# Three reorderings around the stage borders of a state-space, attention and mixture-of-experts kernel

## The chip, the cores and the metric

The kernel runs on one core of a Trainium2 chip. The metric is the device time of one execution in microseconds (us), as the median of several runs. Engine names are those of the profile: PE is TensorE (PEld its weight loads), DVE is VectorE, ACT is ScalarE, POOL is GpSimd, SP is SyncE, which here only issues DMAs.

## What is computed

Two layers, on 4 images of 1024 tokens with 256 channels. Layer 0 normalizes, projects to 512 channels, convolves by depth and runs a state-space recurrence with 64 states a channel along the tokens of each image:

```python
def step(h, inp):
    xt, dtt, Bt, Ct = inp
    dA = jnp.exp(dtt[:, :, None] * A)
    h = dA * h + (dtt * xt)[:, :, None] * Bt[:, None, :]
    y = jnp.einsum('bdn,bn->bd', h, Ct)
    return (h, y)
```

Layer 1 is a linear attention over each image and then a mixture of 16 experts, of which each token uses two, with the weights of their softmax scores:

```python
top_probs, top_idx = jax.lax.top_k(probs, 2)
top_probs = top_probs / jnp.sum(top_probs, axis=-1, keepdims=True)
dispatch = jnp.sum(jax.nn.one_hot(top_idx, n_experts) * top_probs[..., None], axis=-2)
hidden = jax.nn.silu(h1) * h2          # h1 = x @ w1[e], h2 = x @ w2[e]
expert_out = jnp.einsum('bseh,eho->bseo', hidden, w3)
```

## The kernel before

**Stage one, the recurrence** (to about 2698 us of the profiled execution). The work is cut into 8 units (an image's half, 512 tokens) and 64 states a unit, so 512 steps, each of 4 chunks of 128 channels. For each chunk `scan` (L946) runs one VectorE scan over 512 tokens into a ring of four states `h`. After the fourth chunk one GpSimd product (L961) multiplies all four chunks by the state's row of C, 128x2048 at once. `add_up` (L968) lets TensorE transpose the product into the sum `y` in PSUM, four transposes a chunk; it is issued 11 chunks behind the scan (LAG, L1090). The order on every engine is the order in which the loop at L1108 issues: nothing reorders it. After the last chunk `close_sum` (L988) copies `y` out, on VectorE and ACT in turn.

**Stage two, attention** (to about 2943 us). Its first instructions are a memset of `none` on GpSimd (L1240), its store by SP (L1241) and, behind that on SP's queue, the loads of the token tiles `tbs` (L1243 on). The order of this stage is written out by hand, image by image. At its end the expert inputs `xe` of the last image are normalized on ACT (`expert_in`, L1479) and stored by SP into the row table `xd` (L1494), the first three gathers of rows from `xd` are issued on GpSimd (`fetch_rows`, L1776), and the last image's scores are still to be made.

**Stage three, the experts.** Tokens are sorted into blocks of 128 rows, each of one expert. Three blocks an expert are fixed (48); 25 more come from a list made in this stage, and more still would come behind a condition. `blocks_of` (L2050) runs over 73 blocks. For a block: `fetch_rows` gathers its rows (up to seven blocks ahead, `look_ahead`, L2056), `turn_rows` (L1983) transposes them on TensorE (px) and copies them on ACT to xT, `hidden` (L2000) makes two halves of the first products (16 TensorE instructions each, L2008), ACT's Silu and VectorE's product hT (L2015), `result` (L2019) makes the second product, and `put_result` (L2028) scales it and adds it to the output by a scattering DMA from GpSimd. SP loads the experts' weights up to four blocks ahead.

Before the first block, `blocks_of` issues in this order: weight loads, gathers, then `turn_e` (L1496: eight transposes of the first half of xe and two ACT copies to xeT) and `gates` (L1504: four score products and one ACT copy), and then `turn_rows` of the first block.

Between the halves of a block, `on_with` (L1660) advances a chain of generators by four steps (one step after the first eight blocks). A step runs to the next `yield`. The chain is: the second half of the last scores and its routing (`rest_of_routing`, L2095), `spare_rows` (L2109), `more_places` (L2114) and `more_rows` (L2156). `more_places` counts the blocks beyond the fixed ones: `ef` on VectorE, a TensorE transpose of it (L2135), and from that the experts' numbers `eid` (L2136), which SP reads when it loads weights for a listed block. `more_rows` makes the list itself, in eight groups: for each, VectorE compares (`ih`, L2165) and multiplies (`code`, L2171), ACT fills the other half of `code` (L2175), then a `yield`, and eight small TensorE products (L2180) add the group to one PSUM tile. When all are in, `sources` (L1704) turns the sums into row numbers and `choices` (L1717) prepares the weights of the rows.

Of the kernel before, what the change touches and what calls it, by code (L numbers as in the profile page):

```python
# [9 lines left out]
BF16 = mybir.dt.bfloat16  # L10
I32 = mybir.dt.int32
AF = mybir.ActivationFunctionType
ALU = mybir.AluOpType
# [3 lines left out]
P = 128  # L17
BANK = 512
# [15 lines left out]
def conv_ssm_attn_moe_kernel(ctx: ExitStack, tc: tile.TileContext, a: dict, out: bass.AP):  # L34
    nc = tc.nc
# [7 lines left out]
    NE, _, HID = a["L1_ffn_w1"].shape  # L43
    NT = L // P
    NTA = NB * NT
    CK = C // P
    DK = DN // P
# [9 lines left out]
    NMORE = 2 * NB * L // BS - 2 * (FIX - 1)  # L57
# [16 lines left out]
    ident = const.tile([P, P], F32, name="ident")  # L74
# [56 lines left out]
    def blk(i, n=BANK):  # L131
        return slice(i * n, (i + 1) * n)
# [12 lines left out]
    with ExitStack() as l0:  # L145
# [64 lines left out]
        for m in range(DK):  # L210
            for ck in range(CK):
                nc.tensor.matmul(
                    pbi[:, m : m + 1], w_in[:, ck, blk(m, P)], b1[:, ck : ck + 1],
                    start=(ck == 0), stop=(ck == CK - 1),
# [42 lines left out]
        made = {}  # L257
# [616 lines left out]
        steps = [(u, n) for u in range(len(units)) for n in range(NS)]  # L874
# [71 lines left out]
        def scan(s, m):  # L946
            u, n = steps[s]
            b, seg = units[u]
            if m == 0:
                made["h", s] = ring[:, s % RING, :, :]  # L950
            if seg == 0 and n == 0 and m == 0:
                last[b] = acts.tile([P, NS, DK], F32, name="last", bufs=1)
            h = made["h", s]
            nc.vector.tensor_tensor_scan(  # L954
                h[:, m, 1:], made.pop(("da", s, m)), made.pop(("dbx", s, m)),
                0.0 if seg == 0 else last[b][:, n, m : m + 1],
                ALU.mult, ALU.add,
            )
            if m == DK - 1:

                nc.gpsimd.tensor_tensor(  # L961
                    h[:, :, :BANK], h[:, :, 1:], over_middle(made["c", s], DK), ALU.mult
                )
                if seg + 1 < NHALF:
                    with nc.allow_non_contiguous_dma(reason="one element a partition"):
                        nc.sync.dma_start(out=last[b][:, n, :], in_=h[:, :, BANK])
# [126 lines left out]
        with tc.manual_schedule():  # L1093
# [14 lines left out]
            for k in range(n_all + LAG):  # L1108
# [29 lines left out]
                while True:  # L1138
                    best = None
                    for i, l in enumerate(lists):  # L1140
                        if not l or ready[i] + l[0][1] > k or l[0][0] > at and i != holds:
                            continue
                        when, _, eng, c, _, pb, need = l[0]
# [11 lines left out]
                    _, _, eng, c, what, pb, _ = lists[i].pop(0)  # L1155
# [43 lines left out]
    qh = l1.tile([P, 2, NTA, BS], BF16, name="qh")  # L1199
# [493 lines left out]
    eid = late.tile([1, NMORE], I32, name="eid")  # L1693
# [97 lines left out]
    steps = iter(())  # L1791
    for o in range(NB):
        n = o + 1 if o + 1 < NB else None
        z = o - 1 if o > 0 else None
        s = o + 2 if o + 2 < NB else None
# [56 lines left out]
        if z is not None:  # L1852
            turn_g(z)
            steps = route(z)
# [70 lines left out]
    rt2 = ctx.enter_context(tc.tile_pool(name="rt2", bufs=2))  # L1925
# [11 lines left out]
    def one():  # L1937
        return ps_c.tile([P, BANK], F32, name="one", tag="po")
# [44 lines left out]
    def turn_rows(key):  # L1983
        px = ps_x.tile([P, CK, BS], F32, name="px")
        for ck in range(CK):
            nc.tensor.transpose(px[:, ck, :], on_b["xb", key][:, blk(ck, P)], ident)
        xT = ffn.tile([P, CK, BS], F32, name="xT")
        nc.scalar.copy(xT, px)  # L1988
        on_b["xT", key] = xT
# [60 lines left out]
    def blocks_of(todo, beside=(), fast=0, fetched=0):  # L2050

        beside = iter(beside)
        n = len(todo)
        rows = fetched

        def look_ahead(i, deep):  # L2056
            nonlocal rows
            while rows < min(i + deep, n) and todo[rows][0] in given_rows:
                fetch_rows(todo[rows])
                rows += 1  # L2060

        homes.clear()
        held = 0

        def load_ahead(i, gone):
            nonlocal held
            while held < min(i + AHEAD, n) and fetch_weights(todo, held, gone):
                held += 1

        load_ahead(0, 0)  # L2070
        look_ahead(0, AHEAD)
        if fast:
            turn_e(NB - 1, 0)
            gates(NB - 1, 0)
        turn_rows(todo[0])
        for i in range(n + 1):
            if i < n:
                look_ahead(i, 7)
                hidden(todo[i], 0)
            on_with(beside, 4 if i < fast else 1)  # L2080
            if i > 0:
                result(todo[i - 1], 2)
                put_result(todo[i - 1])
            load_ahead(i, i)
            assert i == n or held > i
            if i + 1 < n:
                turn_rows(todo[i + 1])
            if i < n:
                hidden(todo[i], 2)
                weigh(todo[i])  # L2090
                result(todo[i], 0)
            on_with(beside, 4 if i < fast else 1)
        on_with(beside, 99)
# [20 lines left out]
    def more_places():  # L2114

        nbi = rt.tile([P, NE], I32, name="nbi")
        nc.vector.tensor_scalar(nbi, counts[-1], float(BS - 1), None, ALU.add)
        nc.vector.tensor_single_scalar(nbi, nbi, BS.bit_length() - 1, ALU.arith_shift_right)
        nb = rt.tile([P, NE], F32, name="nb")
        nc.vector.tensor_scalar(nb, nbi, -float(FIX), None, ALU.add)  # L2120
        nc.vector.tensor_scalar(nb, nb, 0.0, None, ALU.max)
        nc.vector.tensor_tensor_scan(
            places_to, every[:, :NE], nb, 0.0, ALU.mult, ALU.add
        )
        nc.vector.tensor_scalar(
            used_i, places_to[:, NE - 1 :], 1.0, None, ALU.add
        )
        nc.vector.tensor_tensor(places_of, places_to, nb, ALU.subtract)
        yield
        done = rt.tile([P, NE], F32, name="done")  # L2130
        nc.vector.tensor_scalar(done, places_to, block_p, None, ALU.is_le)
        ef = rt.tile([P, 1], F32, name="ef")
        nc.vector.tensor_reduce(ef, done, AX.X, ALU.add)
        pe = one()
        nc.tensor.transpose(pe[:1, :P], ef, ident)  # L2135
        nc.vector.tensor_scalar(eid, pe[:1, :NMORE], float(NE - 1), None, ALU.min)  # L2136
        yield
        bf = rt.tile([P, 2 * NTA], F32, name="bf")
        for k in range(4):
            pick = rt2.tile([P, NTA // 2, NE], F32, name="pick")  # L2140
            hot = hot_all.rearrange("p k g e -> p (k g) e")[:, blk(k, NTA // 2), :]
            nc.vector.tensor_tensor(pick, hot, over_middle(places_of, NTA // 2), ALU.mult)
            nc.vector.tensor_reduce(bf[:, blk(k, NTA // 2)], pick, AX.X, ALU.add)
            yield
        inside = within.rearrange("p k g -> p (k g)")
        few = rt.tile([P, 2 * NTA], F32, name="few")
        nc.vector.tensor_scalar(
            few, inside, float(FIX), 4.0 * P, ALU.is_lt, ALU.mult
        )
        nc.vector.scalar_tensor_tensor(  # L2150
            bf, inside, -float(FIX), bf, ALU.add, ALU.add
        )
        nc.vector.tensor_tensor(bh, bf, few, ALU.add)
        yield

    def more_rows(lo, hi):  # L2156

        n = hi - lo
        GC = NTA // 4
        pg = one()[:, : 2 * n].rearrange("p (s n) -> p s n", s=2)  # L2160
        for k in range(2):
            for c in range(NTA // GC):
                gs = slice(c * GC, (c + 1) * GC)
                ih = rt2.tile([P, GC, n], BF16, name="ih", tag=f"ih{n}")
                nc.vector.tensor_tensor(  # L2165
                    ih, over_middle(blocks_h[:, lo:hi], GC),
                    over_last(bh[:, k * NTA + c * GC : k * NTA + (c + 1) * GC], n),
                    ALU.is_equal,
                )
                code = rt2.tile([P, GC, 2, n], BF16, name="code", tag=f"code{n}")  # L2170
                nc.vector.tensor_tensor(  # L2171
                    code[:, :, 0, :], ih,
                    over_last(groups[:, c, 0, :], n), ALU.mult,
                )
                nc.scalar.activation(  # L2175
                    code[:, :, 1, :], ih, AF.Copy, scale=part_pk[:, k : k + 1]
                )
                yield
                for j in range(GC):
                    nc.tensor.matmul(  # L2180
                        pg.rearrange("p s n -> p (s n)"), qh[:, k, c * GC + j, :],
                        code[:, j, :, :].rearrange("p s n -> p (s n)"),
                        start=(k + c + j == 0),
                        stop=(k == 1 and (c + 1) * GC + j == NTA + GC - 1),
                    )
        lo, hi = NFIX + lo, NFIX + hi
        nc.vector.tensor_copy(low[:, lo:hi], pg[:, 1, :])
        sources(lo, hi, pg[:, 0, :], low[:, lo:hi])
        given_rows.update(range(lo, hi))
        yield  # L2190
        choices(lo, hi)
        yield
# [57 lines left out]
```

## Time and profile before

| | us |
|---|---|
| Median of 3 runs | 3376.29 (3375.55 to 3376.74) |
| The profiled execution | 3389.96, its span 3387.8 |
| Granted TensorE clock, mean | 0.988 of full |
| Last scan ends, last product of `h` and C starts | 2691.9, 2692.05 |
| First gather issued, first expert product starts | 2943.48, 2951.14 |
| List: first and last group of L2180 start | 2994.3, 3004.9 |
| Last scattering DMA issued | 3376.91 |

Times in a profile count from the span's start. A timeline line gives start, length, engine, line of the code, operation, output and inputs with their shapes, how many instructions are merged, and in brackets how long the engine stood idle before and who ended that. A line of waits gives who waited for whom, the total in us, how often, and the longest. A line of stretches gives the busy time of each engine and the clock that TensorE was granted.

The sum of busy shares is of little use here, since most of the span is stage one: what an edit at a stage border does is read from the timeline there.

### The profile page before, as it was taken

The numbers are of one execution on the slowest core, as the hardware profiler recorded it, in microseconds if no ns is written. First come the engines' busy times: TensorE is split into PE (matmuls) and PEld (weight loads), VectorE is DVE, ScalarE is ACT, GpSimd is POOL, SyncE is SP. The second block draws the span as 40 slices with busy tenths as digits, with TensorE's granted clock in tenths as the row PEclk, the third lists the DMA queues.
The fourth block names the chain that finished last, engine by engine and source line by source line (L and its number), as shares of the span: only waits on it lengthen the run. The fifth ranks groups of instructions, "written<-read, shape, count | busy, mean of one in ns | idle before, by whom it ended". The sixth has DMA issues, their size and how long they took to land. (4 is left out here: it accounts for less than half of the span.)

```text
span 3387.8 us, 62750 instructions
## 1 busy us (share of the span) xinstructions
PE 3172.2 (94%) x23407; PEld 2753.3 (81%) x23407; DVE 2886.9 (85%) x3435; ACT 2717.3 (80%) x4621; POOL 2718.4 (80%) x1215
## 2 busy tenths in 40 slices
PE   7899999999999999999999999989999889789998
PEld 4588888988898888888988988768778756589998
DVE  4699999999999999999999999999999867652222
ACT  1699999999999999999999999899999754322221
POOL 0488998999999989999998999899999842234443
PEclk9999999999999999999999999999999999999999
DMA  3552224224333332253334223423222210467785
GB/s 105 150 68 63 68 66 69 71 71 62 67 78 69 68 72 76 62 63 74 73 73 68 71 64 60 71 54 68 60 62 67 80 48 29 156 186 231 214 245 149
DMA packets 423835, 300.76 MB, mean 89 GB/s; under 512 B 225073, under 2 KB 329393, under 8 KB 423522
## 3 DMA queue, kind: packets, MB, share of 16 engines
q1 hardware_dynamic: 397202, 274.25, 32.9%
q0 software_dynamic: 14016, 18.05, 2.8%
q10 hardware_dynamic: 12304, 4.37, 0.5%
q8 instruction: 187, 3.06, 0.4%
q14 instruction: 126, 1.03, 0.1%
HBM read 262.34 MB, written 34.87 MB: 88 GB/s over the span
## 5 line engine op out<-in xcount | busy, mean ns | idle before, releaser
L961 POOL TENSOR_TENSOR h<-h,cb_n 128x2048 f32<-128x2048 f32 x512 | 2154.9, 4226 | 142.6 <-DVE h L954 89.9
L928 ACT ACTIVATE da<-dt,l_conv_a_log_sb 128x512 f32<-128x512 f32 x2048 | 1438.3, 714 | 32.4 <-DVE h L954 31.3
L908 ACT ACTIVATE bx<-dtxT,proj 128x512 f32<-128x512 f32 x1748 | 1246.9, 714 | 29.9 <-DVE dtxT L600 16.4
L975 PE MATMUL y<-ident,h 128*128 128x128 f32 x8192 | 1236.5, 274 | 8.9 <-POOL h L961 5.8
L954 DVE TENSOR_TENSOR_SCAN h<-da,last,ps 128x512 f32<-128x512 f32 x1024 | 1217.9, 1262 | 7.0 <-PE ps L940 1.8
L954 DVE TENSOR_TENSOR_SCAN h<-da,ps 128x512 f32<-128x512 f32 x1024 | 1169.8, 1201 | 41.8 <-DMA last<-h 16.8
L940 PE MATMUL ps<-ident,bx 128*128 128x128 f32 x6992 | 1119.0, 276 | 41.7 <-DVE h L954 29.4
L975 PEld LDWEIGHTS y<-ident,h 128*128 128x128 f32 x8192 | 979.0, 141 | 99.9 <-issue 20.6
L940 PEld LDWEIGHTS ps<-ident,bx 128*128 128x128 f32 x6992 | 819.7, 142 | 101.8 <-DVE h L954 81.1
L2015 DVE TENSOR_TENSOR hT<-s,p 128x256 f32<-128x256 f32 x146 | 61.4, 421 | 281.0 <-ACT s L2014 281.0
L940 PE MATMUL ps<-ident,bxp 128*128 128x128 f32 x800 | 237.6, 297 | 58.9 <-DVE h L954 46.0
L2033 POOL DMA_INDIRECT out_dram<-yb,src x73 | 116.0, 1589 | 212.3 <-DVE yb L2030 82.2
L2014 ACT ACTIVATE s<-p 128x256 f32<-128x256 f32 x146 | 56.1, 384 | 265.4 <-PE p L2008 262.6
L413 PE MATMUL bg<-pad,dgc 128*128 128x256 f32 x864 | 258.2, 380 | 0.4 <-DMA dgc<-diags 0.4
L940 PEld LDWEIGHTS ps<-ident,bxp 128*128 128x128 f32 x800 | 112.3, 140 | 142.0 <-DVE h L954 89.2
L919 POOL TENSOR_SCALAR bxp<-dtxT,proj 128x512 f32<-128x512 f32 x200 | 147.0, 735 | 59.5 <-DVE dtxT L600 59.5
L935 PE MATMUL ps<-dgb,dtxT 128*128 128x128 f32 x800 | 170.3, 295 | 22.5 <-DMA dgb<-diag_b 9.7
L2008 PE MATMUL p<-xT,w 128*128 128x128 f32 x1408 | 171.7, 275 | 2.2 <-ACT xT L1988 2.2
L2008 PEld LDWEIGHTS p<-xT,w 128*128 128x128 f32 x1408 | 167.4, 192 | 5.0 <-ACT xT L1988 2.9
L935 PEld LDWEIGHTS ps<-dgb,dtxT 128*128 128x128 f32 x800 | 120.5, 190 | 49.2 <-DVE h L954 36.2
L413 PEld LDWEIGHTS bg<-pad,dgc 128*128 128x128 f32 x864 | 130.5, 191 | 0.7 <-DMA dgc<-diags 0.7
L2008 PE MATMUL p<-xT,m 128*128 128x128 f32 x928 | 115.4, 278 | 0.0
(341 smaller groups left out, 2681.6 us busy)
## 6 DMA issues: line engine op xcount, KB each, us to landing
cb_n<-cd SPq DMA_DIRECT2D x512, 256.0 KB, 3.3
m<-in_L_ffn_w_dram SPq DMA_DIRECT2D x87, 512.0 KB, 5.6
w<-in_L_ffn_w_dram SPq DMA_DIRECT2D x60, 512.0 KB, 6.9
dgc<-diags SPq DMA_DIRECT2D x84, 192.0 KB, 3.1
diag_b<-zero SPq DMA_DIRECT2D x2, 4096.0 KB
dgb<-diag_b SPq DMA_DIRECT2D x100, 64.0 KB, 3.2
last<-h SPq DMA_DIRECT2D x256, 2.0 KB, 3.1
xd<-xe SPq DMA_DIRECT2D x8, 512.0 KB, 3.5
```

The lines of the kernel that those rows point to most:

```text
L413: nc.tensor.matmul(made["bg"].rearrange("p (h w) -> p h w", w=WW)[:, blk(c, deep), :], made["dgc", m * 3 + i][:, j, :], pads[m][:, at : at ...
L908: nc.scalar.activation(t, made["dtxT", u][:, j, :], AF.Copy, scale=made["proj", u][:, j, R + n : R + n + 1])
L919: nc.gpsimd.tensor_scalar(t, made["dtxT", u][:, 0, :], made["proj", u][:, 0, R + n : R + n + 1], 1.0, ALU.mult, ALU.mult,)
L928: nc.scalar.activation(t, made["dt", u][:, m, :], AF.Exp, scale=A[:, m, n : n + 1])
L935: nc.tensor.matmul(t[:, blk(j, P)], made["dtxT", steps[s][0]][:, j, blk(m, P)], made["dgb", s], start=True, stop=True,)
L940: nc.tensor.transpose(t[:, blk(j, P)], made["bx", s, j][:, blk(m, P)], ident)
L954: nc.vector.tensor_tensor_scan(h[:, m, 1:], made.pop(("da", s, m)), made.pop(("dbx", s, m)), 0.0 if seg == 0 else last[b][:, n, m : m + 1] ...
L961: nc.gpsimd.tensor_tensor(h[:, :, :BANK], h[:, :, 1:], over_middle(made["c", s], DK), ALU.mult)
L975: nc.tensor.matmul(made["y", u][j][:, blk(m, P)], made["h", s][:, m, blk(j, P)], ident, is_transpose=True, start=n == 0 and m == 0, stop=n ...
L2008: nc.tensor.matmul(p12[:, j, s, :], w_of(w, key)[:, ck, blk(h + j, P)], on_b["xT", key][:, ck, :], start=(ck == 0), stop=(ck == CK - 1),)
L2015: nc.vector.tensor_tensor(on_b["hT", key][:, h : h + 2, :], s, p12[:, :, 1, :], ALU.mult)
L2033: s = nc.gpsimd.indirect_dma_start(of[:, :], bass.IndirectOffsetOnAxis(src[:, c : c + 1], 0), yb, None, bounds_check=NB * L - 1, oob_is_er ...
```

## The change

Three edits. (1) In the last of the 512 steps the product with C is made chunk by chunk, behind each scan: the even chunks on GpSimd, the odd ones on VectorE. (2) In `blocks_of` the first block's rows are transposed ahead of `turn_e` and `gates`. (3) In `more_rows` a group's products are issued three steps behind its code, with five buffers for `code` in place of two and one more `yield`; in `more_places` the transpose for `eid` moves behind the second of the four picks.

```diff
@@ -956,7 +956,11 @@
                 0.0 if seg == 0 else last[b][:, n, m : m + 1],
                 ALU.mult, ALU.add,
             )
-            if m == DK - 1:
+            if s + 1 == len(steps):
+                (nc.vector if m % 2 else nc.gpsimd).tensor_tensor(
+                    h[:, m, :BANK], h[:, m, 1:], made["c", s], ALU.mult
+                )
+            elif m == DK - 1:
 
                 nc.gpsimd.tensor_tensor(
                     h[:, :, :BANK], h[:, :, 1:], over_middle(made["c", s], DK), ALU.mult
@@ -2069,10 +2073,10 @@
 
         load_ahead(0, 0)
         look_ahead(0, AHEAD)
+        turn_rows(todo[0])
         if fast:
             turn_e(NB - 1, 0)
             gates(NB - 1, 0)
-        turn_rows(todo[0])
         for i in range(n + 1):
             if i < n:
                 look_ahead(i, 7)
@@ -2131,9 +2135,6 @@
         nc.vector.tensor_scalar(done, places_to, block_p, None, ALU.is_le)
         ef = rt.tile([P, 1], F32, name="ef")
         nc.vector.tensor_reduce(ef, done, AX.X, ALU.add)
-        pe = one()
-        nc.tensor.transpose(pe[:1, :P], ef, ident)
-        nc.vector.tensor_scalar(eid, pe[:1, :NMORE], float(NE - 1), None, ALU.min)
         yield
         bf = rt.tile([P, 2 * NTA], F32, name="bf")
         for k in range(4):
@@ -2141,6 +2142,12 @@
             hot = hot_all.rearrange("p k g e -> p (k g) e")[:, blk(k, NTA // 2), :]
             nc.vector.tensor_tensor(pick, hot, over_middle(places_of, NTA // 2), ALU.mult)
             nc.vector.tensor_reduce(bf[:, blk(k, NTA // 2)], pick, AX.X, ALU.add)
+            if k == 1:
+                pe = one()
+                nc.tensor.transpose(pe[:1, :P], ef, ident)
+                nc.vector.tensor_scalar(
+                    eid, pe[:1, :NMORE], float(NE - 1), None, ALU.min
+                )
             yield
         inside = within.rearrange("p k g -> p (k g)")
         few = rt.tile([P, 2 * NTA], F32, name="few")
@@ -2153,11 +2160,24 @@
         nc.vector.tensor_tensor(bh, bf, few, ALU.add)
         yield
 
+    LATE = 3
+
     def more_rows(lo, hi):
 
         n = hi - lo
         GC = NTA // 4
         pg = one()[:, : 2 * n].rearrange("p (s n) -> p s n", s=2)
+        behind = []
+
+        def add_rows(k, c, code):
+            for j in range(GC):
+                nc.tensor.matmul(
+                    pg.rearrange("p s n -> p (s n)"), qh[:, k, c * GC + j, :],
+                    code[:, j, :, :].rearrange("p s n -> p (s n)"),
+                    start=(k + c + j == 0),
+                    stop=(k == 1 and (c + 1) * GC + j == NTA + GC - 1),
+                )
+
         for k in range(2):
             for c in range(NTA // GC):
                 gs = slice(c * GC, (c + 1) * GC)
@@ -2167,7 +2187,9 @@
                     over_last(bh[:, k * NTA + c * GC : k * NTA + (c + 1) * GC], n),
                     ALU.is_equal,
                 )
-                code = rt2.tile([P, GC, 2, n], BF16, name="code", tag=f"code{n}")
+                code = rt2.tile(
+                    [P, GC, 2, n], BF16, name="code", tag=f"code{n}", bufs=LATE + 2
+                )
                 nc.vector.tensor_tensor(
                     code[:, :, 0, :], ih,
                     over_last(groups[:, c, 0, :], n), ALU.mult,
@@ -2176,13 +2198,12 @@
                     code[:, :, 1, :], ih, AF.Copy, scale=part_pk[:, k : k + 1]
                 )
                 yield
-                for j in range(GC):
-                    nc.tensor.matmul(
-                        pg.rearrange("p s n -> p (s n)"), qh[:, k, c * GC + j, :],
-                        code[:, j, :, :].rearrange("p s n -> p (s n)"),
-                        start=(k + c + j == 0),
-                        stop=(k == 1 and (c + 1) * GC + j == NTA + GC - 1),
-                    )
+                behind.append((k, c, code))
+                if len(behind) > LATE:
+                    add_rows(*behind.pop(0))
+        yield
+        for one_code in behind:
+            add_rows(*one_code)
         lo, hi = NFIX + lo, NFIX + hi
         nc.vector.tensor_copy(low[:, lo:hi], pg[:, 1, :])
         sources(lo, hi, pg[:, 0, :], low[:, lo:hi])
```

## The prediction

> **What bounds the kernel now.** I read the page's busy shares first, then the stretches by engine from 2940 us on, where two of the three edits act, then TensorE's waits there, and last the timelines around each edit.
>
> ```profile
> PE 3172.2 (94%) x23407; PEld 2753.3 (81%) x23407; DVE 2886.9 (85%) x3435; ACT 2717.3 (80%) x4621; POOL 2718.4 (80%) x1215
> 3100.00:3350.00 250.00, 250.00 (x1903) 238.38 (x1902) 70.23 (x226) 51.72 (x136) 120.37 (x136) 1.00 0.80 232
> PE one L2180 <- ACT code L2175: 4.9, 7, 1.7
> PE pgT L1510 <- ACT xeT L1281: 3.3, 1, 3.3
> ```
>
> The second line is a stretch of the expert stage: length, then busy time of PE, PEld, DVE, ACT, POOL, then granted clock, DMA share, GB/s. TensorE is busy 250.00 of 250 us, at full clock, with no wait on weights. So TensorE's order of work sets the end, and whatever delays it before 3020 us arrives undiminished at the end. The two waits are what the list and the first scores cost it.
>
> The clock is part of the price. The same columns, in 3.41 us stretches:
>
> ```profile
> 2943.54:2946.95 3.41, 0.18 (x1) 0.11 (x2) 0.99 (x6) 2.97 (x7) 2.80 (x3) 1.00 1.01 316
> 2946.95:2950.36 3.41, 3.41 (x5) 0.54 (x4) 0.00 (x0) 0.38 (x2) 0.26 (x1) 0.50 0.41 113
> 2994.74:2998.15 3.41, 1.03 (x25) 1.08 (x26) 2.92 (x11) 1.54 (x5) 2.75 (x3) 1.00 0.43 70
> 2998.15:3001.56 3.41, 3.41 (x20) 3.35 (x18) 0.31 (x1) 0.39 (x1) 0.00 (x0) 0.50 0.15 40
> 3001.56:3004.98 3.42, 1.17 (x29) 1.11 (x28) 2.35 (x7) 1.77 (x4) 0.00 (x0) 0.99 0.00 0
> 3004.98:3008.39 3.41, 3.41 (x19) 2.94 (x19) 1.58 (x7) 0.37 (x1) 0.39 (x1) 0.50 0.02 5
> ```
>
> Each stretch in which TensorE was busy little (0.18, 1.03, 1.17 us) is followed by one at clock 0.50, which costs 1.7 us of a busy TensorE.
>
> **Part 1, the last state (L959).** Removed: one 128x2048 product on GpSimd, started at 2692.05 after the last scan, 4.16 us. TensorE ran out of the state before at about 2693.6, waited 2.69 us, and did the 16 transposes from 2696.27 to 2698.24. Added: chunks 0 and 2 on GpSimd (128x512 products there, L584, take 1287 ns), chunks 1 and 3 on VectorE (687 ns), chunk 1 between the scans of chunks 1 and 2. Undisturbed: GpSimd is free at 2691.55, chunk 0 is ready at 2692.9, chunk 2 at 2694.1. VectorE's scans end 0.69 us later, at 2692.6, and chunk 3 at 2693.3. TensorE runs on at 2693.6 with chunks 0 and 1 (4 transposes each, 0.46 us), takes chunk 2 at 2694.5 and ends at 2695.4: 2.8 us earlier. Behind the inserted product VectorE has only the last two scans, and nobody but TensorE waits for those.
>
> Here a rule speaks against the edit. The Trainium skill (GPSIMD Engine Reference, Specifications) says that GpSimd's SBUF interfaces are shared with VectorE, with contention when a VectorE instruction has two SBUF inputs. The trace agrees:
>
> ```profile
> 2852.34 4.05 DVE L1639 TENSOR_TENSOR qh<-places,qb 128x1024 bf16<-128x1024 bf16 x2
> 2853.60 4.06 POOL L1347 TENSOR_TENSOR tb<-tb,brow 128x256 f32<-128x256 f32 x3
> 2979.45 2.35 DVE L1639 TENSOR_TENSOR qh<-places,qb 128x1024 bf16<-128x1024 bf16 x2
> ```
>
> The same pair took 4.05 us beside GpSimd's products and 2.35 without. If each VectorE product holds GpSimd up for its 0.69 us, the state before ends at 2692.2, chunk 2 at 2695.5 and TensorE at 2696.4: gain 1.9. I take **2.1**, near the contended end, as both VectorE products run beside a GpSimd one; range 1.9 to 2.8. The loads of the next stage (L1243) wait for the memset (L1240), and that for TensorE's last transpose, so the whole next stage starts earlier by as much.
>
> **Part 2, the first gathered rows (L2075).** It issues no DMA; two transposes and one ACT copy pass eight transposes (turn_e), four score products (gates) and three ACT copies. Before, TensorE did turn_e's first half while it waited, the scores next, and the rows last:
>
> ```profile
> 2942.78 0.66 PE L1280 MATMUL ps_t<-ident,xe 128*128 128x128 f32 x4 [1.21 <-DVE tb L1473]
> 2946.77 3.42 PE L1510 MATMUL pgT<-xeT,l_ffn_gate_w_sb 128*16 128x512 f32 x4 [3.33 <-ACT xeT L1281]
> 2950.12 0.55 PE L1986 MATMUL px<-ident,xb_s 128*128 128x128 f32 x2
> 2951.14 1.05 PE L2008 MATMUL p<-xT,w 128*128 128x128 f32 x7 [0.46 <-ACT xT L1988]
> DMA to landing us min/median/max: 5.4/5.4/5.4
> SPq L1494 <- DMA xb_s<-xd,src: 10.4, 1, 10.4
> ```
>
> The last two are the first gather's landing and SP's wait: issued at 2943.48, the gather lands at 2948.9, and SP's store of the rows, which waits for all three gathers, goes at 2949.7, which fits. So the transposes now put first cannot start before 2948.9. Behind them on TensorE stand turn_e and the scores, which need no gather; behind the copy on ACT stand turn_e's copies, which the scores need. From 2948.9 TensorE has rows 0.38, turn_e 1.04 (L1280, eight of them) and scores 1.89 (L1510's second run, at full clock): 3.3 us, and the expert products start at 2952.2 at the earliest, 1.1 late. But TensorE has then been idle from 2941.6 on. At half clock throughout it would be 6.6 us, 4.4 late. With one half-clock stretch of 3.4 us it is 3.3 + 1.7, 2953.9. I take a loss of **2.8**, range 1.1 to 4.4; the row at 2946.95 says that the half clock is due. What the edit removes is the 0.46 us wait for xT, already in this sum. If the gather landed by 2946 the loss would be about nil. The routing of the last batch, the longest VectorE chain here, hangs behind these scores, so it moves as one.
>
> **Part 3, the list.** Before, each of eight groups of products stands right behind its own code:
>
> ```profile
> 2996.36 0.36 PE L2180 MATMUL one<-code,qh 128*128 128x50 bf16 x8 [1.67 <-ACT code L2175]
> 2998.05 3.65 PE L2008 MATMUL p<-xT,m 128*128 128x128 f32 x16
> 3003.46 0.36 PE L2180 MATMUL one<-code,qh 128*128 128x50 bf16 x8 [1.55 <-ACT code L2175]
> ```
>
> From the first group (2994.32) to the score products of the block after next (about 3010.5) it takes 16.2 us. Work at full clock, start to start: two score halves of 1.79, two result halves of 0.87, rows 0.21, eight groups of 0.36: 8.4. Waits on codes 4.7 (4.9 less the first 0.2); the rest, 3.1, is the half clock, near the 3.4 of two stretches.
>
> After: in this call four codes are made and only the first group issued; the second to fifth groups follow the next score half, the last three a half block later. Codes 2 to 5 are ready at 2996.30, 2997.07, 2997.80 and 2998.54 (ACT's code operations in the timeline). TensorE reaches the second group at 2996.5, so about 0.3 us of wait stays before each of groups 3, 4 and 5: 1.0 in all. The last three find their codes done. VectorE and ACT do the same code operations in the same order; hT and the next xT fall behind three codes, but each is ready (2999.4, 3002.0) before TensorE asks (3001.8, 3003.8). That gives 9.4 us, a gain of 6.8.
>
> Here rule and row part. The Trainium skill (TensorE: Matmul & The Clock Gate, HAM oscillation — how this bites in real kernels) warns of TensorE gaps above about 3.4 us. No single gap among the list's products reaches 1.7 us, so by it no clock comes back: 6.8 - 3.1, gain 3.7. The rows show two half-clock stretches after 1.03 and 1.17 us of work, so scattered gaps count. But such a stretch must lie badly on the 3.41 us raster, and the timed runs need not lie as this profile did. I take **5.5**, nearer the rows; range 3.3 to 6.8.
>
> The rest costs nothing. The eid transpose stands in the same call, with no TensorE work between its old and new place; TensorE still waits 2.1 us for ef, and VectorE's 0.36 us wait for it was covered. The three extra code buffers are memory. The list comes one call later, but look_ahead reads it at the next block in both cases, and SP reads the first eid at 3019.6; were that cover gone, a half block, 2.8 us, would be lost.
>
> **Sum.** -2.1 + 2.8 - 5.5 = -4.8. The profiled execution took 3389.96 us (span 3387.8 and 2.2 around), so 3385.2 there; its steps are the same in the timed runs, whose median is 13.7 less: 3376.3 - 4.8 = **3371.5**. A measurement of this kernel can tell about 0.2%, 6.8 us, from no change, so faster begins at 3369.5 and slower at 3383.0.
>
> **Rivals.**
> - *Both half-clock stretches go and the gather costs little*: part 3 at 6.8, part 2 at 1.5 (undisturbed clock), part 1 at 2.8: -8.1, 3368.2. For it: the two rows at 0.50. Against it: TensorE's idle 7 us before the gather. Chance 0.37, anything from 3365 to 3369.5.
> - *The list's waits only change places*: the codes come every 0.75 us whatever TensorE does, so if VectorE's order holds the result halves up too, 2 us stays: -2.8 + 2 = about -1, 3375.5. Against it: the ready times above. Chance 0.07.
> - *Slower: the gather at the head of TensorE's queue.* Each us that it lands later than 2948.9 is paid in full, as scores and experts stand behind it. It decides from 5 us later (2953.9); from 11.6 us on the kernel is slower by over 0.2%. At 12 us: 3376.3 + 7.2 = 3383.5. For it: it shares the DMA engines with a 1 MB store. Against it: gathers land in 2.8 to 7.5 us in the whole stage. Chance 0.06.
>
> My forecast, 3369.5 to 3375, has 0.50. Faster is 0.37; forecast and second rival, 0.57, lie within 0.2%; slower is 0.06. The range 3366.0 to 3376.5 leaves out part of the first rival and the last.
>
> **What would show it.** Right: chunk products at 1.3 and 0.7 us or somewhat above and TensorE's last transpose 2 to 3 us after the last scan; the first expert products 2 to 4 us later against the last out products, with the scores behind px; TensorE's wait for code about 1 us and clock 1.00 where the list is made. Wrong: a gather that lands before turn_e would have run, or a TensorE that waits elsewhere before 3020 us, or is no longer fully busy after it.

## The result, and the profile after

The changed kernel takes **3365.71 us** (median of 8 runs, 3364.59 to 3368.74), the kernel before in the same session 3375.64 (8 runs, 3375.08 to 3379.85). The ratio is 0.9971, 95% interval 0.9961 to 0.9981: 9.9 us faster, somewhere between 6.4 and 13.2. The forecast was 3371.5; the result lies 0.3 us below the lower end of its range, where the first rival (both half-clock stretches go and the gather costs little) stood.

The profiled execution has a span of 3363.1 us, before 3387.8. Of these 24.7 us, 15.0 lie in stage one, which the change doesn't touch: the scan of the state before last ends at 2687.2 before and at 2672.2 after. Over all the profiles of this study this point lies anywhere from 2671 to 2687, with the same instructions ahead of it, and the timed medians show no such step. So I count every profile from there: 700.61 us to the end before, 690.86 after, a difference of 9.75 that agrees with the timed 9.9, more closely than the interval can confirm. By stage (a block's first products are made in two halves, which the prediction also calls score halves; "scores" here are the last image's expert scores):

| us | before | after | difference | predicted |
|---|---|---|---|---|
| Border: to TensorE's last y transpose | 11.00 | 8.66 | -2.34 | -2.1 |
| Loads and attention, to the first gather's issue | 245.24 | 244.64 | -0.60 | 0 |
| Gather's issue to the first expert product | 7.66 | 8.51 | +0.85 | +2.8 |
| From there to the list's first group | 43.18 | 43.10 | -0.08 | 0 |
| List, to the first products of the block after next | 16.23 | 8.71 | -7.52 | -5.5 |
| The rest | 377.29 | 377.24 | -0.05 | 0 |

TensorE is still what sets the end. The same stretch of the expert stage as before, in the same columns (length, busy PE, PEld, DVE, ACT, POOL, clock, DMA share, GB/s), with the list's stretches ahead of it:

```profile
2977.20:2980.61 3.41, 2.90 (x45) 2.84 (x45) 3.00 (x11) 1.79 (x5) 2.66 (x3) 1.00 0.47 105
2980.61:2984.02 3.41, 3.10 (x36) 2.92 (x35) 2.74 (x10) 2.03 (x6) 0.01 (x1) 1.00 0.25 57
...
3100.00:3350.00 250.00, 250.00 (x1903) 238.34 (x1901) 70.23 (x226) 51.24 (x135) 117.12 (x134) 1.00 0.75 217
```

Where the list is made TensorE is now busy 2.90 and 3.10 us of 3.41, in place of 1.03 and 1.17, and both half-clock stretches are gone. TensorE's waits in the expert stage:

```profile
PE px L1990 <- DMA xb_s<-xd,src: 7.6, 1, 7.6
PE one L2147 <- DVE ef L2137: 2.0, 1, 2.0
PE one L2174 <- ACT code L2197: 1.0, 4, 0.3
```

The wait on codes fell from 4.9 us to 1.0. The wait on xeT (3.3) is gone, and the whole idle time before the experts stands now at the gather (7.6). How the list lies on TensorE, from the timeline:

```profile
2977.11 0.36 PE L2174 MATMUL one<-code,qh 128*128 128x50 bf16 x8 [0.18 <-ACT code L2197]
2977.37 2.05 PE L2012 MATMUL p<-xT,m 128*128 128x128 f32 x16
...
2980.50 0.36 PE L2174 MATMUL one<-code,qh 128*128 128x50 bf16 x8 [0.32 <-ACT code L2197]
...
2985.20 0.78 PE L2174 MATMUL one<-code,qh 128*128 128x50 bf16 x24
```

The half of the first products that took 3.65 us takes 2.05, the longest wait is 0.32, and the last three groups run as one of 0.78. The start of the expert stage, in the same view:

```profile
2929.56 0.66 PE L1990 MATMUL px<-ident,xb_s 128*128 128x128 f32 x2 [7.59 <-DMA xb_s<-xd,src]
2930.01 1.92 PE L1284 MATMUL ps_t<-ident,xe 128*128 128x128 f32 x8
2931.86 2.22 PE L1514 MATMUL pgT<-xeT,l_ffn_gate_w_sb 128*16 128x512 f32 x4
2934.01 2.05 PE L2012 MATMUL p<-xT,w 128*128 128x128 f32 x16
```

The gather, issued at 2925.50, landed 3.9 us later. From the landing to the first expert product it took 4.6 us, most of it at half clock (1.92 where the eight transposes take 1.04 at full clock). And the border on VectorE:

```profile
2674.58 2.48 DVE L960 TENSOR_TENSOR h<-h,cb_n 128x512 f32<-128x512 f32 x1
...
2679.46 0.69 DVE L960 TENSOR_TENSOR h<-h,cb_n 128x512 f32<-128x512 f32 x1
```

The same product takes 2.48 us between the scans and 0.69 behind the last one.

### The profile page after: what moved, and what is told of

It is laid out like the page before. It is cut to its first block, busy times and chain, and to the rows that moved or that the text cites. A ratio compares the mean times of both kernels' runs of the same rounds, so it can differ in the third digit from the quotient of the medians.

```text
span 3363.1 us, 62751 instructions
## 1 busy us (share of the span) xinstructions
PE 3159.0 (94%) x23407; PEld 2745.3 (82%) x23407; DVE 2889.3 (86%) x3437; ACT 2716.1 (81%) x4621; POOL 2716.9 (81%) x1216
## 3 DMA queue, kind: packets, MB, share of 16 engines
q14 instruction: 126, 1.03, 0.1%
## 5 line engine op out<-in xcount | busy, mean ns | idle before, releaser
L940 PE MATMUL ps<-ident,bxp 128*128 128x128 f32 x800 | 236.5, 296 | 52.3 <-DVE h L954 40.7
```

The lines of the kernel that those rows point to most:

```text
L940: nc.tensor.transpose(t[:, blk(j, P)], made["bx", s, j][:, blk(m, P)], ident)
```

## The experiments

**My theory** after the result: the three parts add up; the list gave more than I took because its half clock belongs to the schedule and not to one profile; the rows first cost less because the gather landed early. **The rival**: the parts help each other (less idle time in one place moves the clock in another), or the list's clock was an accident. The durations below come from the profiles, counted as above; ratios are against the kernel before on the same chip.

### Each part alone, and the change without the rows

e1 to e3 are the kernel before with one part of the diff each; e4 is the changed kernel with this undone:

```diff
-        turn_rows(todo[0])
         if fast:
             turn_e(NB - 1, 0)
             gates(NB - 1, 0)
+        turn_rows(todo[0])
```

> Only the last state's products are made chunk by chunk; the rest is the kernel before. My theory (the changed kernel's profile: last scan of the state before to TensorE's last transpose 8.7 us in place of 11.0): 2.3 us faster than before, carried whole to the end. Rival (the border is covered by the loads that follow): under 1 us.

> Only the first block's rows are turned ahead of the last image's scores. My theory: TensorE stands before the gather with the scores behind it, so about 1 us slower (0.3 to 2.8). Rival, that the reordering is a gain: 0.5 us or more faster. The profile should show the rows' transposes ahead of the scores and the first expert products 8 us or more after the first gather's issue; before it was 7.7.

> Only the list's products run three steps behind their codes (with the moved transpose for eid). My theory: 7.5 us faster, of which 4 come from waits and 3 from two half-clock stretches. Rival (the two half-clock stretches were an accident of the profiled execution and are not in the timed ones): 4 us faster.

> The changed kernel with the first rows back behind the scores. My theory: 10.7 us faster than before, 0.9 us faster than the changed kernel. Rival, that the reordering gains: 9.4 or less.

| | border | gather's issue to experts | to the list | list | all from the border on | ratio (95%) |
|---|---|---|---|---|---|---|
| before | 11.00 | 7.66 | 43.18 | 16.23 | 700.61 | |
| after | 8.66 | 8.51 | 43.10 | 8.71 | 690.86 | 0.9971 |
| e1, last state | 8.66 | 7.92 | 43.12 | 16.18 | 699.83 | 0.9997 (0.9988 to 1.0006) |
| e2, rows first | 11.01 | 9.12 | 43.18 | 16.12 | 701.24 | 1.0005 (0.9997 to 1.0013) |
| e3, list | 11.82 | 6.54 | 44.76 | 8.71 | 696.77 | 0.998 (0.9972 to 0.9988) |
| e4, without rows first | 8.67 | 6.66 | 44.76 | 8.71 | 691.31 | 0.9968 (0.9956 to 0.998) |

The parts are read stage by stage. The totals of single profiles don't add up (0.8, -0.6 and 3.8 us for 9.75), since stages that an edit doesn't touch differ as well: over the profiles, loads and attention take 244.4 to 248.5 us, and e3's border, with its code as before, 11.82. The medians do: 2.3 us for e1 and 6.8 for e3, against 9.2 for e4, which has both, though each with an interval of several us.

The list's 7.5 us are there alone as with the other parts (8.71 in each of these kernels with the new list, 16.1 to 16.2 with the old), and it is the only part that a timed run shows by itself: 3377.27 against 3384.07, 6.8 us, with an interval of 4.1 to 9.5. The border's 2.3 is the same in e1 and after, but the ratio of e1 doesn't reach beyond no change. e2 is unclear by the timed runs as well; its profile loses 1.5 us at the gather. e4 is as fast as the full change: without the rows first, gather to list takes 51.4 us, with them 51.6.

e1 has the old list in another session and with another start of the stage. Its stretches there:

```profile
2985.50:2988.90 3.40, 1.08 (x25) 1.12 (x26) 2.96 (x11) 1.53 (x5) 2.74 (x3) 1.00 0.48 89
2988.90:2992.30 3.40, 3.40 (x20) 3.34 (x20) 0.26 (x1) 0.35 (x1) 0.00 (x0) 0.51 0.14 39
2992.30:2995.70 3.40, 1.20 (x32) 1.12 (x30) 2.35 (x7) 1.77 (x4) 0.00 (x0) 0.99 0.00 0
2995.70:2999.10 3.40, 3.40 (x20) 2.94 (x17) 1.58 (x7) 0.37 (x1) 0.52 (x1) 0.51 0.00 0
```

Little work, half clock, little work, half clock, as in the kernel before. The first half-clock stretch begins 3.9, 3.9 and 3.6 us behind the list's first group in before, e1 and e2. So it came back with this order of work. But the three lists lie alike on the 3.41 us raster of the clock, within 0.3 us, so that it would come at another place too is not shown.

e4's timeline shows why it is no faster than the full change although its experts start earlier:

```profile
2936.45 3.60 PE L1514 MATMUL pgT<-xeT,l_ffn_gate_w_sb 128*16 128x512 f32 x4 [3.34 <-ACT xeT L1285]
...
2941.13 3.75 PE L2012 MATMUL p<-xT,w 128*128 128x128 f32 x16 [0.46 <-ACT xT L1992]
```

The wait for xeT is back, the scores run at half clock, and here so does the first expert half (3.75 for 2.05), which is the 1.7 us by which e3 and e4 come later to the list. In before, e1, e5 and e10, which have the same order, that half ran at full clock. So the rows first give back at the clock what they take at the gather in these two profiles only, by luck. From the gather's issue to the list the old order took 50.8 to 51.5 us (before, e1, e3 to e5), the new one 51.6 in the change, profiled twice, and 52.3 in e2: never less.

### The list's waits filled, its order kept (e5)

The kernel before, with transposes of the identity into a tile that nobody reads, ahead of each group's products:

```diff
+        fill = one()
...
                 yield
+                for _ in range((0, 12, 3, 3, 0, 12, 3, 3)[k * 4 + c]):
+                    nc.tensor.transpose(fill[:, :P], ident, ident)
                 for j in range(GC):
```

> The kernel before, with transposes that nobody reads (12, 3 and 3 of 0.11 us) in TensorE's waits ahead of the second to fourth and the sixth to eighth group of the list's products. The waits stay, TensorE is busy in them. My theory, that scattered waits bring the half clock: no stretch at 0.50 in the list, list stretch (first group to the score products of the block after next) from 16.2 to about 13 us, kernel 3 us faster than before. Rival, that the half clock has another cause or costs nothing: 16.2 us, or a little more, and no faster.

The list took 12.97 us. From its timeline:

```profile
2997.09 1.51 PE L2181 MATMUL one<-ident 128*128 128x128 f32 x12
2998.93 0.36 PE L2183 MATMUL one<-code,qh 128*128 128x50 bf16 x8 [0.33 <-ACT code L2176]
...
3000.61 2.03 PE L2008 MATMUL p<-xT,m 128*128 128x128 f32 x16
```

The groups still come when their codes come, but the half of the first products behind them takes 2.03 us where it took 3.65, and no stretch of the list is at 0.50. This separates the two terms: 3.3 us of the 7.5 were the clock, brought back by work that is of no use, and the other 4.3 the waits. The timed ratio, 0.9996 (0.9986 to 1.0006), doesn't show the 3.3; in the profile attention took 3.7 us longer than before (231.27 for 227.58, from its first query and key products to the gather's issue), so the profile's total doesn't either. The split rests on the list's own stretch.

### The border, the store, the eid transpose (e6 to e8)

e8 takes all four chunks of the last product to VectorE, behind its last scan:

```diff
-                (nc.vector if m % 2 else nc.gpsimd).tensor_tensor(
-                    h[:, m, :BANK], h[:, m, 1:], made["c", s], ALU.mult
-                )
+                for i in range(DK if m == DK - 1 else 0):
+                    nc.vector.tensor_tensor(
+                        h[:, i, :BANK], h[:, i, 1:], made["c", s], ALU.mult
+                    )
```

> The changed kernel with all four chunk products of the last state on VectorE, behind the last scan, none on GpSimd. Theory, that VectorE's product took 2.48 us only because GpSimd's running product held it: four products of 0.7 us, TensorE's last transpose 8.0 us after the scans of the state before (8.7 in the changed kernel). Rival, that this product is slow by itself: 2 us or more each, 12 us or more.

```profile
2681.84 5.93 DVE L954 TENSOR_TENSOR_SCAN h<-da,last,ps 128x512 f32<-128x512 f32 x5
2687.69 2.46 DVE L961 TENSOR_TENSOR h<-h,cb_n 128x512 f32<-128x512 f32 x4
```

Four products take 2.46 us in sequence, less than the one inserted product took beside GpSimd. The border is 8.08 us, 0.6 below the change's. Why is seen on GpSimd in the changed kernel:

```profile
2672.34 4.17 POOL L965 TENSOR_TENSOR h<-h,cb_n 128x2048 f32<-128x2048 f32 x1 [0.52 <-POOL h L965]
2676.46 2.96 POOL L960 TENSOR_TENSOR h<-h,cb_n 128x512 f32<-128x512 f32 x2
```

GpSimd's running product ends at 2676.51, VectorE's inserted one, begun at 2674.58, at 2677.06: VectorE stood until GpSimd was done. The big product itself took its usual 4.17. As a whole e8 is no faster than the change: 694.17 us from the border on for 690.86, ratio 0.9972 (0.9961 to 0.9982), because of its gather (below) and of a half-clock stretch behind the wait for `ef`.

e7 issues the last image's 1 MB store (the rows with the attention added) from ACT behind `expert_in` in place of ahead of it; the gather was meant to find the DMA engines free:

```diff
-        nc.scalar.dma_start(out=rows(of, o), in_=tbs[o])
+        if n is not None:
+            nc.scalar.dma_start(out=rows(of, o), in_=tbs[o])
         if n is None:
...
             expert_in(o, 1)
+            nc.scalar.dma_start(out=rows(of, o), in_=tbs[o])
```

> The changed kernel with the 1 MB store of the last image's tokens issued behind ACT's last four normalizations, so 3 us later and behind the first gather's issue. Theory, that the gather's landing is set by the store ahead of it: it lands 3 us after its issue (3.9 in the changed kernel) and the first experts start 0.9 us earlier. Rival, that the landing is the gather's own cost: 3.9 us again, no gain.

It went the other way: the first gather landed after 5.6 us, not earlier than 3.9, the experts started 10.85 us behind the issue, and the ratio is 0.9976 (0.9965 to 0.9987). The store then comes 0.5 us behind the gather and moves beside it. Over all profiles in which the first gather's landing is seen, it lands sooner, in the main, the longer the store's lead:

| | store issued ahead of the gather, us | gather lands after, us |
|---|---|---|
| e7 | -0.5 | 5.6 |
| e5 | 0.3 | 5.1 |
| e8 | 0.5 | 5.3 |
| before | 0.7 | 5.4 |
| e10 | 1.7 | 3.8 |
| after, e9 | 1.7 | 3.9, 3.7 |
| e6, e11 | 2.1, 2.0 | 3.5, 4.3 |
| e12 | 2.9 | 3.0 |

Of these, e7 alone was made to move the store; the rest is order seen, not set. What makes the lead can be read from the traces. The gather goes 1.2 us after the small store of `xe` (SP) has landed, in all ten profiles of the table. The 1 MB store goes when VectorE has added the last out product: 2.65 us behind the issue of that small store in eight profiles, 2.9 in e2, but 4.0 to 4.3 in before, e1, e5 and e8. In these four, and in e7, TensorE has a half-clock stretch of 6.8 us late in attention, and VectorE has to wait for its out products. In the kernel before:

```profile
2937.54 0.48 DVE L1473 SCALAR_TENSOR_TENSOR tb<-po,rq,tb 128x256 f32<-128x256 f32 x1 [0.90 <-PE po L1469]
2939.27 0.48 DVE L1473 SCALAR_TENSOR_TENSOR tb<-po,rq,tb 128x256 f32<-128x256 f32 x1 [0.26 <-PE po L1469]
```

Whether the stretch comes is decided just ahead of it, by where the same work falls on the clock's raster: first the kernel before, then the changed one.

```profile
2926.50:2929.91 3.41, 1.52 (x6) 0.68 (x4) 3.19 (x8) 1.12 (x2) 1.47 (x1) 1.00 0.18 70
2929.91:2933.33 3.42, 2.12 (x5) 1.76 (x6) 3.28 (x9) 0.00 (x0) 0.00 (x0) 0.50 0.00 0
...
2908.67:2912.09 3.42, 1.81 (x8) 0.99 (x6) 3.14 (x10) 1.12 (x2) 1.35 (x1) 1.00 0.30 116
2912.09:2915.50 3.41, 1.82 (x9) 1.53 (x9) 3.31 (x7) 0.00 (x0) 0.12 (x1) 1.00 0.00 0
```

With 1.1 to 1.6 us of TensorE work in that stretch the next was at 0.50, in six profiles (in e2 for 3.4 us only); with 1.75 to 1.8 it was at 1.00, in eight. So the 5.4 us of the kernel before belonged to a profile with this stretch, and the changed kernel's profile escaped it by luck, since the change doesn't touch the place. e7 and e8 have the change and the stretch: their gathers took 5.6 and 5.3 us, and their experts start 10.85 and 10.95 us behind the issue, 3.2 and 3.3 more than before, near the 2.8 of the prediction. As e7 has the stretch too, it doesn't show alone what moving the store does.

e6 moves the eid transpose one call on:

```diff
-            if k == 1:
+            if k == 2:
```

> The changed kernel with the transpose for eid behind the third pick in place of the second, so that it falls into the next call. My theory (in the change the transpose stayed in the same call, with no TensorE work between its old and new place): TensorE's wait of 2.0 us for ef goes, 2 us faster than the changed kernel. Rival, that TensorE then waits as long elsewhere because VectorE's chain of routing is late: no faster, the stretch from the first experts to the first list group stays 43.1 us.

```profile
PE one L2174 <- ACT code L2197: 1.9, 4, 1.0
...
PE one L2147 <- DVE ef L2137: 0.4, 1, 0.4
```

The wait for ef falls from 2.0 to 0.4, but TensorE then comes earlier to the codes and waits 0.9 longer there. 0.8 us remains from the experts' start to the list (42.32 for 43.10), the whole is 690.93 against 690.86, and the ratio, 0.9965 (0.9952 to 0.9977), overlaps the change's. The wait itself isn't always free: in e8 it left a stretch with 1.3 us of TensorE work, the next was at 0.50, and the list came 1.7 us later (44.77 us behind the first experts).

### The rows first with a busy TensorE, and all together (e9 to e12)

e9 is the changed kernel again, on the chip of the other three. e12 adds 55 transposes of the identity ahead of the first `turn_rows`, so that TensorE isn't idle while the gather is under way:

```diff
+        fill = ps_x.tile([P, CK, BS], F32, name="px")
+        for _ in range(55 if fast else 0):
+            nc.tensor.transpose(fill[:, 0, :], ident, ident)
         turn_rows(todo[0])
```

> The changed kernel once more, beside the next three on one chip. Theory: 0.997 of the time of before, as in the result, with the list stretch at 8.7 us and the first experts 8.2 to 11 us after the first gather's issue, by when that gather lands (3.5 to 5.6 us so far).

> The changed kernel with 55 transposes that nobody reads (6.2 us) ahead of the first block's rows, so that TensorE is busy until the gather lands. My theory of the price of rows first (landing, then rows, transposes and scores in a row, at half clock): the first experts start 3.5 us after the landing in place of 4.6, 1 us faster than the changed kernel. Rival, that the clock has no part in it: 4.6 us as before.

```profile
2930.98 1.04 PE L1284 MATMUL ps_t<-ident,xe 128*128 128x128 f32 x8
2932.25 1.89 PE L1514 MATMUL pgT<-xeT,l_ffn_gate_w_sb 128*16 128x512 f32 x4 [0.24 <-ACT xeT L1285]
2934.07 2.05 PE L2012 MATMUL p<-xT,w 128*128 128x128 f32 x16
```

All at full clock, and 3.5 us from the landing to the experts where the changed kernel took 4.6: the half clock there is 1.1 us. The kernel as a whole got nothing of it: 691.13 against 691.02 for e9, ratios 0.997 (0.9958 to 0.9983) and 0.9972 (0.9963 to 0.9981). Its gather was issued 1.1 us later in attention (228.30 for 227.17).

e10 joins what had helped: e8's border, the rows back behind the scores, e6's transpose, and five steps of lateness in the list (`LATE = 5`). e11 is e10 with 28 such transposes between `turn_e` and `gates`.

> The changed kernel with all four last products on VectorE, the first rows back behind the scores, the list's products five steps behind their codes and the eid transpose in the next call. My theory: border 8.1 us (8.7 changed), first experts plus routing 50 us (51.6), no wait on codes, together 2 to 3 us faster than the changed kernel. Rival, that the rows first are worth something once the rest is in place: no faster than the changed kernel.

> The combined kernel with 28 transposes that nobody reads (3.2 us) in TensorE's wait ahead of the first scores. Theory, that the half clock at the scores comes from that wait: scores in 1.9 us in place of 3.4, the first experts bound by the gather's landing, 1 to 3 us faster than the combined kernel. Rival, that the scores' few columns alone bring the half clock: no change.

| | experts behind the gather's issue | all from the border on | median | ratio (95%) |
|---|---|---|---|---|
| e9, the change | 8.45 | 691.02 | 3368.1 | 0.9972 (0.9963 to 0.9981) |
| e10 | 7.03 | 686.75 | 3364.56 | 0.9961 (0.9947 to 0.9974) |
| e11 | 5.34 | 686.51 | 3361.28 | 0.9957 (0.9943 to 0.997) |

```profile
2923.49 3.22 PE L2081 MATMUL px<-ident 128*128 128x128 f32 x28
2926.99 1.89 PE L1515 MATMUL pgT<-xeT,l_ffn_gate_w_sb 128*16 128x512 f32 x4 [0.28 <-ACT xeT L1286]
2929.45 0.41 PE L1991 MATMUL px<-ident,xb_s 128*128 128x128 f32 x2 [0.57 <-DMA xb_s<-xd,src]
```

In e11 the scores (1.89 us) fit into the time that the gather takes, and the experts start 1.7 us earlier behind the issue than in e10; but the gather itself was issued 1.0 later. Both beat the kernel before, and e11 is the fastest measured (15.3 us below the 3376.58 of before in that session). Over the changed kernel the profiles give 4.3 and 4.5 us, the medians 3.5 and 6.8, and the intervals overlap. Of e10's 4.3, 0.6 lies at the border, 0.3 in attention, 1.4 from the gather's issue to the first experts, and 2.0 behind them, where the list and the eid transpose stand. In e10 and e11 TensorE no longer waits for a code at all.

## Why the prediction was right or wrong

The parts and their signs were right. Two terms failed on size: part 3's discount on the half clock, and part 2's landing of the gather. Together they make 4.0 of the 5.8 us by which the forecast missed.

**What bounds the kernel: right.** TensorE stays fully busy from 3100 to 3350 us, and what was saved before 3020 arrives: the rest after the list differs by 0.05 us of 377.

**Part 1: right.** -2.34 for -2.1, inside the range of 1.9 to 2.8. The reason was only half right: I let each VectorE product hold GpSimd up for its 0.69 us. GpSimd's two chunks took 1.72 and 1.09 us where the row said 1.29, but the larger delay was VectorE's, 1.8 us on its inserted product, and with it on the two scans behind it. So the path was not the predicted one: TensorE's last transposes waited for VectorE's last product (to 2680.15), not for GpSimd's second chunk (to 2679.42). That the gain fell near the 2.1 is in part luck.

**Part 2: the mechanism right, the size off.** +0.85 for +2.8, below the range of 1.1 to 4.4. The order foreseen is there: rows, `turn_e`, scores, experts, in one piece behind the landing, with the half clock. The mis-sized term is the landing, "it lands at 2948.9", 5.4 us from the issue, which I took over as it stood in one profile; it took 3.9. That is 1.5 of the 1.95 us; the other 0.4 is the work behind it, 4.6 us for the 5.0 of the sum. With a landing of 5.3 (e8) the loss is 3.3. So the small loss of the result is luck of its profile, which had no half-clock stretch late in attention; how many of the timed runs had it isn't known. The prediction had a cause in hand (the gather shares the DMA engines with a 1 MB store) and used it only for the rival that ends slower; the table says that it works both ways.

**Part 3: the step that failed is the discount.** The sum by the rows was 6.8. Then: "But such a stretch must lie badly on the 3.41 us raster, and the timed runs need not lie as this profile did. I take **5.5**". Measured: 7.52 in the profile, 6.8 in the timed runs of e3, whose interval (4.1 to 9.5) holds the 5.5 too, so it is the profiles that decide. The half-clock stretches stood at the same place of the list in all three profiles with the old list at hand, and e5 priced them at 3.3 us, where the sum by the rows had 3.1. The rule of the Trainium skill (TensorE: Matmul & The Clock Gate, HAM oscillation — how this bites in real kernels), weighed there with 3.7, is the one that misled here: it counts only gaps above about 3.4 us, and no gap in the old list reaches 1.7. The remaining wait on codes, worked out at 1.0, was 1.0. The whole came to 0.7 more than the rows gave: 0.2 of it is the clock, and 0.3 the last three groups, at 0.78 together and not three times 0.36.

**The rest costs nothing: right.** The eid transpose still waits 2.0 us for ef where it stands; nothing behind it moved. The remaining -0.60 is attention and its loads. The half-clock stretch late in attention, present before and absent after, lies in it; as e7 and e8 have it with the change, I don't count it to the change.

**The sum.** -2.34 + 0.85 - 7.52 is -9.0, and -9.75 with attention and the small terms; timed -9.9. Of the 5.8 us by which the forecast missed, part 3 makes 2.0, part 2 1.95, attention and the small terms 0.7 and part 1 0.2; 0.65 is that the kernel before stood at 3375.64 and not at 3376.29 this time, and 0.2 is left between profile and timed runs. The small terms are far below what the timed runs can tell. The first rival, -8.1, named both errors and was given 0.37. The other two didn't occur: TensorE's wait on codes went down rather than over to the result halves, and the gather landed earlier, not later.

**What stays open.** In e4 a stretch in which TensorE was busy 2.94 of 3.40 us, mostly with the score products of 16 columns, lies at 0.50 itself and is followed by another at 0.50; e3 has the same. In e10 the same products in the same order fill as much, and the next stretch is at 1.00:

```profile
2937.90:2941.30 3.40, 2.94 (x6) 0.61 (x5) 0.00 (x0) 1.15 (x3) 0.30 (x1) 0.50 0.22 66
...
2932.38:2935.79 3.41, 2.95 (x6) 0.46 (x4) 0.00 (x0) 1.00 (x3) 0.09 (x1) 0.50 0.31 99
2935.79:2939.20 3.41, 3.41 (x31) 3.41 (x32) 0.42 (x1) 2.52 (x4) 0.00 (x0) 1.00 0.92 277
```

So neither the products' shape nor the busy share, as the profile gives it, explains the clock there. Nor is it known how often the timed runs have the stretch late in attention, or how part 2 would then come out in them.

## What to carry to other kernels

When an order of work leaves the matrix engine busy only about a third of a clock stretch (here 0.97 to 1.30 us of 3.41), price the lost clock as part of the wait: it came back in each profile of that order, and dummy work in the gaps is a cheap test of the price. A DMA's landing time from one profile is valid only beside the traffic of that moment: before putting work behind it at the head of a queue, look at what was issued around it, and at whether the clock in that profile delayed that traffic, and cost it at both ends. And before splitting a product between two vector engines to save time, try giving it whole to the faster one: here four products one behind the other took less than one beside the other engine.

## What the runs showed of the hardware

- TensorE's clock was granted in stretches of 3.41 us, and went with the busy share of a stretch more than with the longest gap. In the list, stretches with 0.97 to 1.30 us of TensorE work in short pieces, no gap over 1.7 us, were followed by one at 0.50 in before, e1 and e2; where the list keeps TensorE busy 2.90 us of 3.41, the clock stays at 1.00. Late in attention 1.1 to 1.6 us were followed by 0.50 and 1.75 to 1.8 by 1.00, mostly with the same longest gap, 1.6 us.
- It is no sharp limit: in e6 a stretch with 1.45 us (at 2881.7) was followed by 1.00, in e5 one with 1.72 us (at 2942.8) by 0.50, and e4 and e10 part at the same 2.9 us at half clock.
- A VectorE product of 128x512 with two SBUF inputs, begun while GpSimd was in a product of 128x2048, took 2.48 us for 0.69 and ended 0.55 us after GpSimd's did.
- The gather landed after 3.0 to 5.6 us, in the main sooner the longer the 1 MB store had been under way before it (an order seen over ten profiles).
